# Building the FFN matrix from mirrored columns, in a cross-attention and Fourier-FFN kernel: a rewritten first row group

## The chip, the core and the metric

The kernel runs on one core of a Trainium2 chip. The core has five engines with instruction queues of their own, which run in order and meet only at semaphores: TensorE (PE in the profile, with PEld for its weight loads), VectorE (DVE), ScalarE (ACT), GpSimd (POOL) and SyncE (SP), which here only issues transfers (DMAs). The metric is the device time of one execution in microseconds (us). Everything is in float32.

## The reference

Two residual blocks over `x` of shape (2, 2048, 512), with a context of (2, 128, 512):

```python
x = x + xattn(layernorm(x), ctx, mask, wq, bq, wk, bk, wv, bv, wo, bo)
x = x + ffn(layernorm(x), w_freq_real, w_freq_imag, bias)
```

The cross-attention has 16 heads of 32. Scores are scaled, multiplied by the mask, and set to -1e9 where the product is zero; then softmax over 128 keys, the weighted values, and the output projection. The FFN works on frequencies:

```python
y = real(ifft(fft(x) @ (w_real + 1j * w_imag))) + bias
```

This is linear in `x`, so it is one real 512 x 512 matrix applied to each row. The kernel computes that matrix on the chip, from the two weight matrices and cosine and sine tables, and then uses it as an ordinary weight.

## The kernel before, in words

**Tiling.** The 4096 rows are eight groups of 512 (`GQ`), each of four tiles of 128. Group i, tile t is written (i,t). One tile's attention is a "slot" (`slot`, L687): the scores of 16 heads in two halves of eight (`scores`, L297; matmul L307), then for each half the mask multiply (`masked`, L326), the compare and the row minima (`maxima`, L333 to L336) on VectorE, eight exponentials with sums on ScalarE (`exponentials`, L342), a reciprocal on VectorE and the division on GpSimd (`divided`, L354, L355). TensorE transposes the divided weights one tile later (`transposed_weights`, L368), in two halves of eight transposes, and ScalarE copies them out (L375).

**What fills TensorE.** A slot takes three "chains": products of 128 rows by 512 columns summed over four chunks (`chain`, L192 to L199; its matmul is L196 whatever the product is). Chains make queries (`q`), values (`v`), the output projection (`o`), the FFN (`y`), and, in the first groups, the two steps that build the FFN matrix (`half`, `m`). Group i's slots carry the queries of the next group, the projection of group i-1 and the FFN of group i-2.

**What sets the order.** The program's order is written out by hand (a manual schedule): each engine's queue holds its instructions in the order in which the Python code issues them. Tiles of on-chip memory come from pools with few buffers, and an instruction that takes a buffer waits for its last user. Those that matter here: `ps_mm` ("mm", two buffers for the results of chains), `ps_tp` ("tp", two, for transposes), `ps_sc` ("sc", two, the halves of a tile's scores), `rel` (four, one for each row tile of a group).

**The start.** SyncE issues all loads in one order: context, rows of group 0, key and query bias, wq, rows of group 1, the mask of group 0, the FFN weights wr and wi, wv, the tables (`dft`), wo (L139 to L178 of the code). `keys` (L507) transposes the context and forms the keys, with "busy" transposes of the identity (L505) before and between; ScalarE evicts the keys (L547). Rows are reduced to differences from their first element (`relative`, L228), reduced to statistics (`query_statistics`, L203 to L208), normalized (`query_norm`, L211) and transposed (`query_transposes`, L186). Then TensorE makes all four query chains of group 0 (`Queries`, the first in two halves of 256 columns at L276), with three folds between, before the first scores.

**The FFN matrix.** `FoldRows` (L585) adds and subtracts the rows of wr and wi whose frequencies mirror each other: one matmul with a flipped identity (L597), up to four operations on VectorE (L604 to L611). `fold_columns` (L615) does the same for columns, with four 510-wide VectorE operations, one operand of each read backwards (L628), and four copies of an unpaired column (L629). `Half` (L631) multiplies these columns with the tables, four chains of 512 columns; `FfnMatrix` (L655) multiplies the result with the tables again, four more. Each is evicted by one ScalarE instruction (L651, L668). The row without a mirror partner sits in the place of the sine row that is zero: L856 sets that row of the table to ones. The two `half` tables' columns are the even (cosine) and odd (sine) functions of the column number.

Group 0 runs in the same loop as groups 1 to 5: values and queries of group 1 in its slots 0 and 1, `half` in slots 2 and 3, `m` from slot (0,3) to (1,1).

Of the kernel before, what the change touches and what calls it, by code (L numbers as in the profile page):

```python
# [9 lines left out]
FP = mybir.dt.float32  # L10
# [12 lines left out]
def kernel(  # L23
# [130 lines left out]
    nc.sync.dma_start(wq, chunks(wq_w))  # L154
    load_rows(1)
    load_mask(0)
# [35 lines left out]
    def chain(name, lhs, rhs):  # L192

        ps = ps_mm.tile([P, D], FP, tag="mm", name=name)
        for c in range(NC):
            nc.tensor.matmul(  # L196
                ps, lhs(c), rhs(c), start=(c == 0), stop=(c == NC - 1)
            )
        return ps  # L199
# [30 lines left out]

    def query_statistics(i, first, end):
# [23 lines left out]
    class Queries:  # L255
        def __init__(self, i, g):
            self.i, self.g = i, g

        def pe(self):
            i, g = self.i, self.g  # L260
            if g == 0:
                qTs[i] = big_tile("qT", 2, f"qT_{i}")
            if i > 0 or g > 0:
                self.ps = chain(
                    f"q_{i}_{g}",
                    lambda c: wq[:, c, g * P : (g + 1) * P],
                    lambda c: xnTs[i][:, c, :],
                )
                return


            self.ps = ps_mm.tile([P, GQ], FP, tag="mm", name="q_0_0")
            for h in range(2):
                qs = slice(h * GQ // 2, (h + 1) * GQ // 2)
                for c in range(NC):
                    nc.tensor.matmul(  # L276
                        self.ps[:, qs],
                        wq[:, c, :P],
                        xnTs[i][:, c, qs],
                        start=(c == 0),  # L280
                        stop=(c == NC - 1),
                    )

        def evict(self):
            nc.scalar.activation(  # L285
                qTs[self.i][:, self.g, :],
                self.ps,
                AF.Identity,
                bias=bq[:, self.g : self.g + 1],
            )  # L290
# [210 lines left out]
    def busy(count):  # L501

        ps = ps_tp.tile([P, NC, P], FP, tag="tp", name=f"busy_{count}")
        for k in range(count):
            nc.tensor.transpose(ps[:, k % NC, :], ident, ident)  # L505

    def keys():  # L507
# [11 lines left out]
        busy(2)  # L519
# [25 lines left out]
        def evict():  # L545
            for g in range(NC):
                nc.scalar.activation(  # L547
                    kT[:, g, :],
                    ps[g],
                    AF.Identity,  # L550
                    bias=bk[:, g : g + 1],
                    scale=SCALE / UNIT,
# [4 lines left out]
    class Values:  # L557
# [13 lines left out]
        on_vector = True  # L571

# [42 lines left out]
    def fold_columns():  # L615
# [4 lines left out]
        for k, (x1, x2, op, first) in enumerate(  # L620
# [7 lines left out]
            nc.vector.tensor_tensor(cols[:, k, :, 1:], x1, x2, op)  # L628
            nc.vector.tensor_copy(cols[:, k, :, 0:1], first)  # L629

    class Half:  # L631


        def __init__(self, what, g):
            self.what, self.g = what, g

        def pe(self):
            what, g = self.what, self.g
            self.ps = chain(
                f"half_{what}_{g}",  # L640
                lambda i: cols[
                    :,
                    2 * what + i // HC,
                    HC - 1 - i if i < HC else i - HC,
                    g * P : (g + 1) * P,
                ],
                lambda i: dft[:, i, :],
            )

        def evict(self):  # L650
            nc.scalar.copy(half[:, self.what * HC + self.g, :], self.ps)  # L651

        on_vector = False

    class FfnMatrix:  # L655
        def __init__(self, g):
            self.g = g

        def pe(self):
            g = self.g  # L660
            self.ps = chain(
                f"m_{g}",
                lambda i: half[:, i, g * P : (g + 1) * P],
                lambda i: dft[:, i, :],
            )

        def evict(self):
            nc.scalar.mul(m_ffn[:, self.g, :], self.ps, 1.0 / D)  # L668

        on_vector = False  # L670
# [110 lines left out]
    evict_biases()  # L781
    for t in range(TG):
        query_transposes(0, t)
        relative(1, t, nc.gpsimd)
    evict_keys()
    query_statistics(1, 0, TG)
    for t in range(TG):
        query_norm(1, t)
# [5 lines left out]
    for g in range(NC):  # L794
        run(Queries(0, g))
        if g > 0:
            run(folds[g - 1])

    halves_of = [Half(what, g) for what in range(2) for g in range(HC)]
    m = [FfnMatrix(g) for g in range(NC)]  # L800
    none = [None] * TG

    for i in range(last - 1):
# [3 lines left out]
        o = [Project(p, t) for t in range(TG)] if p >= 0 else none  # L807
        f_pp = [Ffn(pp, t) for t in range(TG)] if pp >= 0 else none
        f_p = Ffn(p, 0) if p >= 0 else None
        if i == 0:  # L810
            first, second = [Values(0), Values(1), q[0]], [q[1], q[2], q[3]]
            third, fourth = halves_of[:3], [halves_of[3], m[0], q_nn]
        else:
            if i == 1:
                first, second = [m[1], m[2], q[1]], [q[2], q[3], m[3]]
            else:
                first, second = [f_pp[1], f_pp[2], q[1]], [q[2], q[3], f_pp[3]]
            third, fourth = o[:3], [o[3], f_p, q_nn]

        def behind(*work):  # L820
            return list(work) if p >= 0 else []

        def before(*work):
            return list(work) if pp >= 0 else []

        load_rows(nn)
        load_mask(n)
        call(before((load_residual, p)))
        slot(
            i,  # L830
            0,
            first,
            turned=(p, TG - 1) if p >= 0 else None,
            early=(
                [(query_transposes, n, t) for t in range(TG)]
                if i == 0
                else before((ffn_transposes, pp, 1), (ffn_transposes, pp, 2))
            ),
            pool=[(relative, nn, t, nc.gpsimd) for t in range(TG)],
            on_b=before((ffn_norm, pp, 3)) + [(query_statistics, nn, 0, 2)],  # L840
            on_c=[(query_statistics, nn, 2, TG)],
            end=[(run, folds[3])] if i == 0 else [(context, p, 0, 2)],
        )
# [5 lines left out]
            early=behind((context, p, 2, NC)) + before((ffn_transposes, pp, 3)),  # L849
            pool=behind((output_bias, p)) if p > 0 else [],  # L850
            on_b=[(query_norm, nn, 0), (query_norm, nn, 1)]
            + ([(fold_columns,)] if i == 0 else []),
        )
        if i == 0:
            load_residual(0)
            nc.vector.memset(dft[0:1, HC, :], 1.0)  # L856
# [3 lines left out]
            third,  # L860
            turned=(i, 1),
            early=[(query_transposes, nn, 0), (query_transposes, nn, 1)],
            pool=behind((output_bias, p)) if p == 0 else [],
            on_b=behind((ffn_statistics, p, 0))
            + [(query_norm, nn, 2), (query_norm, nn, 3)]
            + behind((ffn_norm, p, 0)),
# [179 lines left out]
```

## Time and profile before

| what | value |
|---|---|
| median of three runs | 555.21 us (555.14 to 557.09) |
| the profiled execution | 557.46 us, span of its instructions 555.5 us |
| DVE, ACT, POOL busy | 430.3 us (77%), 344.0 us (62%), 316.3 us (57%) |
| share of PE in the chain that ended last | 81% |
| scores of (0,0), (0,1), (0,2), (0,3) begin | 35.38, 50.10, 63.46, 77.64 us |
| scores of (1,0), (1,1), (1,2) begin | 91.82, 107.42, 122.63 us |
| division of a half's weights on POOL (L355) | 1921 ns, 64 times |
| bias added to a row tile on POOL (L406) | 1520 ns, 32 times |

A group of instructions in the profile is one line, engine, operation and pair of tiles; it comes with its busy time, the mean of one instruction, and what ended the idle time before it. Matmul records overlap in TensorE's pipeline, so a busy PE row says that something was in flight, and the price of a matmul is better read from the starts of consecutive rows in the timeline. Records count two for one float32 matmul; a transpose is one.

### The profile page before, as it was taken

The page shows a single profiled execution, that of the slowest core. Times are in us where ns is not written, and L with a number is a line of the kernel's source. Part 1 is how long each engine was busy: PE and PEld are TensorE (multiplying, and loading weights), DVE is VectorE, ACT ScalarE, POOL GpSimd, SP SyncE. Part 2 cuts the span into 40 slices and gives each one's busy share as a digit, 9 for nine tenths or more (in the row PEclk, how much of TensorE's full clock was granted, in tenths as well). Part 3 has the DMA queues.
Part 4 walks back from the last instruction along what each step waited for, and adds up shares of the span by engine and source line. Part 5 has one row for each costly group of instructions (what it writes and reads, how often), then busy time and mean ns, then how long its engine had stood idle before and what let it go on. Part 6 is the DMA issues. An engine that isn't in the chain of part 4 may idle for free.

```text
span 555.5 us, 8688 instructions
## 1 busy us (share of the span) xinstructions
PE 543.2 (98%) x2975; PEld 291.4 (52%) x2975; DVE 430.3 (77%) x613; ACT 344.0 (62%) x1295; POOL 316.3 (57%) x248
## 2 busy tenths in 40 slices
PE   8999999999999999999999999999999999998997
PEld 7654555455554555455545555455545555454444
DVE  4468986669997898879898898879857898798251
ACT  3325777876766666777666666677776666666200
POOL 3534224727697268944696259935645466855450
PEclk9999999999999999999999999999999999999999
DMA  8950130000150005000230006000310201201102
GB/s 325 378 187 2 48 104 21 0 1 1 35 194 0 21 1 197 31 6 14 99 129 1 21 1 209 21 19 1 114 38 23 73 2 58 94 2 38 40 0 76
DMA packets 22735, 36.47 MB, mean 66 GB/s; under 512 B 1946, under 2 KB 6306, under 8 KB 22692
## 3 DMA queue, kind: packets, MB, share of 16 engines
q1 hardware_dynamic: 22004, 34.75, 18.0%
q10 hardware_dynamic: 688, 1.18, 0.6%
q8 instruction: 23, 0.38, 0.3%
q14 instruction: 20, 0.16, 0.1%
HBM read 27.53 MB, written 8.39 MB: 65 GB/s over the span
## 4 chain that ended last, share of the span: by engine, by line
PE 81%; DVE 10%; ACT 6%; issue 1%; DMA 1%; POOL 1%; SPq 0%; ACTq 0%; DVEq 0%; POOLq 0%
PE q L196 18%; PE y L196 16%; PE o L196 15%; PE tpw L368 8%; PE sc L307 5%; PE c L390 5%; ACT w L342 4%; DVE w L333 3%; PE half L196 2%; DVE nmax L335 2%; PE tp_a L186 2%; PE tp_f L186 2%; PE m L196 2%; DVE w L326 2%; PE k L533 2%; PE v L196 1%
## 5 line engine op out<-in xcount | busy, mean ns | idle before, releaser
L342 ACT ACTIVATE w<-w,nmax 128x128 f32<-128x128 f32 x512 | 198.3, 396 | 16.6 <-DVE nmax L336 14.7
L355 POOL TENSOR_TENSOR w<-w,rden 128x1024 f32<-128x1024 f32 x64 | 123.0, 1921 | 144.0 <-DVE rden L354 81.7
L196 PE MATMUL o<-wo,cT 128*128 128x512 f32 x256 | 115.1, 594 | 0.0
L196 PE MATMUL y<-m_ffn,nT 128*128 128x512 f32 x248 | 112.3, 596 | 2.1 <-DVE nT L190 1.0
L196 PE MATMUL q<-xnT,wq 128*128 128x512 f32 x248 | 112.1, 594 | 0.0
L375 ACT COPY pt<-tpw 128x512 f32<-128x512 f32 x124 | 66.7, 587 | 65.0 <-PE tpw L368 65.0
L342 ACT ACTIVATION_READ_ACCUMULATOR w<-w,nmax 128x1 f32 x512 | 99.5, 194 | 0.0
L333 DVE SCALAR_TENSOR_TENSOR w<-w 128x1024 f32<-128x1024 f32 x64 | 89.1, 1393 | 1.0
L326 DVE TENSOR_TENSOR w<-sc,mask 128x1024 f32<-128x1024 f32 x64 | 77.5, 1212 | 9.5 <-PE sc L307 9.0
L335 DVE TENSOR_REDUCE nmax<-w 128x8 f32<-128x1024 f32 x64 | 78.1, 1220 | 2.2
L368 PEld LDWEIGHTS tpw<-ident,w 128*128 128x128 f32 x512 | 59.5, 141 | 36.0 <-issue 31.2
L196 PEld LDWEIGHTS o<-wo,cT 128*128 128x128 f32 x256 | 46.3, 190 | 47.9 <-issue 46.6
L196 PEld LDWEIGHTS y<-m_ffn,nT 128*128 128x128 f32 x248 | 44.7, 190 | 48.3 <-issue 44.8
L368 PE MATMUL tpw<-ident,w 128*128 128x128 f32 x512 | 67.9, 274 | 2.0 <-ACT nT L188 1.0
L196 PEld LDWEIGHTS q<-xnT,wq 128*128 128x128 f32 x248 | 44.8, 190 | 47.6 <-issue 44.7
L445 POOL TENSOR_TENSOR x<-x,bf 128x512 f32<-128x512 f32 x32 | 48.9, 1528 | 18.0 <-DVE norm_f L211 18.0
L228 POOL TENSOR_SCALAR rel<-rows 128x512 f32<-128x512 f32 x28 | 46.7, 1681 | 15.1 <-PE tp_a L186 15.1
L354 DVE RECIPROCAL rden<-den 128x8 f32<-128x8 f32 x64 | 12.7, 199 | 54.2 <-ACT w L342 54.1
L406 POOL TENSOR_TENSOR x<-x,bo 128x512 f32<-128x512 f32 x32 | 47.6, 1520 | 0.0
L307 PEld LDWEIGHTS sc<-kT,qT 32*128 32x128 f32 x1024 | 31.4, 186 | 22.4 <-issue 20.0
L285 ACT ACTIVATE qT<-q,bq 128x512 f32<-128x512 f32 x32 | 21.7, 678 | 32.0 <-PE q L196 30.5
L207 POOL TENSOR_SCALAR rstd_f<-mv_f 128x1 f32<-128x1 f32 x32 | 19.9, 623 | 34.8 <-DVE mv_f L204 34.8
(81 smaller groups left out, 526.2 us busy)
## 6 DMA issues: line engine op xcount, KB each, us to landing
rows<-in_x_dram SPq DMA_DIRECT2D x32, 256.0 KB, 4.5
x<-in_x_dram SPq DMA_DIRECT2D x32, 256.0 KB, 4.9
out_dram<-x SPq DMA_DIRECT2D x31, 256.0 KB, 2.0
mask<-in_mask_Bx1xSxS_fk_dram SPq DMA_DIRECT2D x8, 256.0 KB, 4.8
wk<-in_L_xattn_wk_w_dram ACTq DMA_DIRECT2D x2, 512.0 KB, 6.5
wq<-in_L_xattn_wq_w_dram SPq DMA_DIRECT2D x1, 1024.0 KB, 7.2
wr<-n_L_ffn_w_freq_real_dram SPq DMA_DIRECT2D x2, 512.0 KB, 5.3
wi<-n_L_ffn_w_freq_imag_dram SPq DMA_DIRECT2D x2, 512.0 KB, 6.6
```

The lines of the kernel that those rows point to most:

```text
L196: nc.tensor.matmul(ps, lhs(c), rhs(c), start=(c == 0), stop=(c == NC - 1))
L228: eng.tensor_scalar(d, xt, xt[:, 0:1], None, ALU.subtract)
L307: nc.tensor.matmul(sc[r // 2][:, r % 2, g, :], qTs[i][rows, g, t * P : (t + 1) * P], kT[rows, g, b * K : (b + 1) * K], start=True, stop=True,)
L326: nc.vector.tensor_tensor(self.w, self.sc.rearrange("p r g k -> p (r g) k"), self.mrow, ALU.mult)
L333: nc.vector.scalar_tensor_tensor(w, w, 0.0, w, ALU.is_equal, ALU.subtract)
L335: nc.vector.tensor_reduce(self.nmax, w, AX.X, ALU.min)
L342: nc.scalar.activation(w[:, h, :], w[:, h, :], AF.Exp, bias=self.nmax[:, h : h + 1], scale=-UNIT, accum_out=self.den[:, h : h + 1],)
L355: nc.gpsimd.tensor_tensor(w, w, rden.unsqueeze(2).to_broadcast([P, HH, K]), ALU.mult)
L368: nc.tensor.transpose(ps[:, r, :], ws[r // 2].w[:, (r % 2) * NC + g, :], ident)
L375: nc.scalar.copy(dst, ps)
L406: nc.gpsimd.tensor_tensor(xs[:, t, :], xs[:, t, :], bo, ALU.add)
L445: nc.gpsimd.tensor_tensor(xt, xt, bf, ALU.add)
```

## The change

- **Mirrored sums.** `Half` and `FfnMatrix` become one class, `Mirrored`. Of each chain of four matmuls, two make the even part (257 columns) and two the odd part (255). ScalarE evicts the even part with a bias and the odd part to a tile of its own; two operations then form the columns above 256, backwards, as even minus odd, and the columns below as even plus odd. They run on GpSimd for seven of the eight sums and on VectorE, from the accumulator, for the fourth `half`.
- **The unpaired row.** It is now a bias for each partition. Four transfers of 128 elements gather the row into a [4, 128] tile, TensorE transposes it and ScalarE copies it, once for `half` and once for `m`. The row of ones in the table is gone.
- **Columns.** `fold_columns` runs on GpSimd, in tile (0,2). The first `half` stands in tile (0,3) instead of (0,2), and the last `m` in (1,0) instead of (1,1). The projection of group 0 begins in (1,2) as before.
- **Queries ahead.** The queries of the first tile alone (128 columns) stand before the first scores; the other 384 columns of group 0 follow in tile (0,0). Row tile 3 is transposed after the first queries.
- **Order at the start.** Keys are evicted by VectorE. Two of group 1's subtractions move from GpSimd to VectorE. The mask of group 0 is loaded ahead of the rows of group 1. Two filler transposes after the context's become three after each half of it, in the "mm" pool.
- **Group 0 and slot (1,0)** are written out one by one. Folds stand in tiles (0,0) and (0,1). In (1,0), the first two weight copies and the first two context evictions go to VectorE. The loop runs from group 1, and its code from slot (1,1) on is what it was, but for the three chains of (1,1), now q_1, q_2, q_3.

```diff
-    load_rows(1)
     load_mask(0)
+    load_rows(1)
...
+    def first_queries(i, g):
...
+        ps = chain(
+            f"q_{i}_{g}_first",
+            lambda c: wq[:, c, g * P : (g + 1) * P],
+            lambda c: xnTs[i][:, c, :P],
+            width=P,
+        )
...
+        nc.scalar.activation(
+            qTs[i][:, g, :P], ps, AF.Identity, bias=bq[:, g : g + 1]
+        )
...
-                nc.scalar.activation(
+                nc.vector.tensor_scalar(
                     kT[:, g, :],
                     ps[g],
...
-            nc.vector.tensor_tensor(cols[:, k, :, 1:], x1, x2, op)
-            nc.vector.tensor_copy(cols[:, k, :, 0:1], first)
+            nc.gpsimd.tensor_tensor(cols[:, k, :, 1:], x1, x2, op)
+            nc.gpsimd.tensor_copy(cols[:, k, :, 0:1], first)
...
+    def load_first_rows(name, pieces):
+
+        rows = small.tile([NC, P], FP, tag="rows0", bufs=2, name=name)
+        for k, piece in enumerate(pieces):
+            nc.sync.dma_start(rows[k : k + 1, :], piece)
+        return rows
+
+    def first_rows(name, rows, scale):
+
+        ps = ps_tp.tile([P, NC], FP, tag="tp", name=f"ps_{name}")
+        nc.tensor.transpose(ps, rows, ident[:NC, :NC])
+        add = small.tile([P, NC], FP, tag="add", bufs=2, name=name)
+        nc.scalar.mul(add, ps, scale)
+        return add
+
+    class Mirrored:
...
+        def pe(self):
+            ps = ps_mm.tile([P, D], FP, tag="mm", name=self.name)
+            self.even, self.odd = ps[:, : HD + 1], ps[:, HD + 1 :]
+            for i in range(NC):
+                nc.tensor.matmul(
+                    self.even if i < HC else self.odd,
+                    self.lhs(i),
+                    dft[:, i, : HD + 1] if i < HC else dft[:, i, 1:HD],
+                    start=(i % HC == 0),
+                    stop=(i % HC == HC - 1),
+                )
+
+        def evict(self, add, eng=nc.gpsimd):
+            low, high = self.dst[:, 1:HD], self.dst[:, D - 1 : HD : -1]
+            nc.scalar.activation(
+                self.dst[:, : HD + 1],
+                self.even,
+                AF.Identity,
+                bias=add,
+                scale=self.scale,
+            )
+            odd = self.odd
+            if eng is nc.gpsimd:
+                odd = work.tile([P, HD - 1], FP, tag="odd", name=f"odd_{self.name}")
+                nc.scalar.mul(odd, self.odd, self.scale)
+            eng.tensor_tensor(high, low, odd, ALU.subtract)
+            eng.tensor_tensor(low, low, odd, ALU.add)
...
+    for t in range(TG - 1):
+        query_transposes(0, t)
+    evict_keys()
     for t in range(TG):
...
+        relative(1, t, nc.gpsimd if t < 2 else nc.vector)
+    query_statistics(1, 0, TG - 1)
+    for g in range(NC):
+        first_queries(0, g)
+    query_transposes(0, TG - 1)
...
+    w = begin(0, 0)
+    w[0].masked()
+    run(rest[0])
+    w[0].maxima()
+    query_statistics(1, TG - 1, TG)
+    w[0].exponentials()
+    w[1].masked()
+    run(rest[1])
+    run(rest[2])
+    w[1].maxima()
+    w[1].exponentials()
+    run(rest[3])
+    for t in range(TG):
+        query_norm(1, t)
+    w[0].divided()
+    run(folds[0])
+    w[1].divided()
+    run(folds[1])
...
+    w = begin(0, 2)
+    w[0].masked()
+    fold_columns()
+    rows_h = load_first_rows("rows_h", [x.lhs(HC)[0:1, :] for x in h])
+    load_residual(0)
...
+    w = begin(0, 3)
+    w[0].masked()
+    q[2].evict()
+    w[0].maxima()
+    add = first_rows("add_half", rows_h, 1.0)
+    for k in range(HC):
+        h[k].pe()
+        h[k].evict(add[:, k : k + 1])
+    transposed_weights(0, 2, 0, HC)
+    w[0].exponentials()
+    w[1].masked()
...
+    h[2].pe()
+    h[2].evict(add[:, 2:3])
+    rows_m = load_first_rows("rows_m", [x.lhs(HC)[0:1, :] for x in m])
+    h[3].pe()
+    h[3].evict(add[:, 3:4], nc.vector)
+    transposed_weights(0, 2, HC, NC)
+    w[1].exponentials()
+    w[0].divided()
+    run(q[3])
+    m[0].pe()
+    add = first_rows("add_m", rows_m, 1.0 / D)
+    m[0].evict(add[:, 0:1])
+    w[1].divided()
```

## The prediction, made before the changed kernel was run

> **What bounds the kernel now.** I read the page first, then the groups by shape in the first 140 us, the timeline of PE, the waits of PE, and small windows for the first matmuls. The page:
>
> ```profile
> span 555.5 us, 8688 instructions
> ...
> PE 543.2 (98%) x2975; PEld 291.4 (52%) x2975; DVE 430.3 (77%) x613; ACT 344.0 (62%) x1295; POOL 316.3 (57%) x248
> ...
> PE   8999999999999999999999999999999999998997
> ```
>
> PE is busy from end to end, and in the first 140 us its waits are few:
>
> ```profile
> PE tp_enc L513 <- DMA enc<-in_ctx_dram: 0.6, 1, 0.6
> PE tp_a L186 <- ACT xnT L188: 0.5, 2, 0.3
> ...
> PE c L390 <- ACT qT L285: 0.2, 1, 0.2
> ```
>
> So PE work taken out of the start shortens the span, until another queue is late. The groups of that stage (columns: busy us, mean ns | idle before):
>
> ```profile
> L196 PE MATMUL m<-dft,half 128*128 128x512 f32 x32 | 14.5, 596 | 0.0
> L196 PE MATMUL half<-dft,cols 128*128 128x512 f32 x32 | 14.4, 593 | 0.0
> ...
> L276 PE MATMUL q<-xnT,wq 128*128 128x256 f32 x16 | 3.6, 379 | 0.0
> ...
> L333 DVE SCALAR_TENSOR_TENSOR w<-w 128x1024 f32<-128x1024 f32 x14 | 19.8, 1417 | 0.4
> ...
> L211 DVE TENSOR_SCALAR rel<-rel,mv,rstd 128x512 f32<-128x512 f32 x16 | 13.0, 856 | 1.9 <-POOL rstd L208 1.9
> ...
> L628 DVE TENSOR_TENSOR cols<-wr 128x510 f32<-128x510 f32 x2 | 1.4, 677 | 0.0
> ```
>
> Matmul records overlap, so their mean is not their price; that is the distance between starts, read from the timeline of PE:
>
> ```profile
> 18.58 3.62 PE L276 MATMUL q<-xnT,wq 128*128 128x256 f32 x16
> 22.03 3.60 PE L196 MATMUL q<-xnT,wq 128*128 128x512 f32 x8
> ```
>
> Sixteen records of 256 columns take 3.45 us (0.216 each); eight of 512 take 25.47 - 22.03 = 3.44 (0.43 each). Time goes with columns. The kernel's records are two per fp32 matmul, so a chain of four is eight records.
>
> **PE's saving.** Eight chains (four half, four m) go from 512 columns to 257 and 255: 8 x 0.216 = 1.73 us for 3.44. That is 8 x 1.71 = 13.7 us. Two small transposes of the unpaired row add 0.1 each. The split queries cost nothing: 4 x (8 x 0.109, the spacing of 128-column transposes) + 4 x (8 x 0.323) = 13.8, against 3.45 + 3 x 3.44 = 13.8. Net 13.5 us, if nothing waits.
>
> **The new order, walked queue by queue.** Both kernels have done the same work where the scores of tile (1,2) begin: 122.63 in the trace of before (q_1 of group 2 has moved behind, m_3 ahead). I price PE's work from the end of the keys (16.3) to there: scores 1.10, half a tile's weight transposes 0.87, four transposes 0.45, a fold 0.86, two context groups 1.85. For before the prices sum to 103.5, with 0.7 of waits; the trace has 106.3. The missing 2.1 are joints (a chain behind scores takes 3.63, not 3.44); the new order has as many, so I add 2.1 to it too. The other queues: DVE 3.8 for one half's mask, compare and reduce; 0.87 for a row tile's statistics; ACT 3.1 for eight exponentials, 0.55 to 0.7 for a 512-wide eviction.
>
> *To the first scores.* Transposes of three tiles and a wait for ACT (0.4): 18.1. First queries 3.5, tile 3's transpose 0.45: scores at 22.2, against 35.4. The key evictions move to DVE, 4 x 0.42, done by 18.1, covered by the first queries; without that cover they would cost 1.7. DVE has a new wait: the subtraction for row tile 3 of group 1 takes a buffer that PE frees with tile 3's transpose (22.1). Three statistics (2.6) and then the first mask multiply are queued behind it, so softmax begins at 25.2, not 23.3.
>
> *Tile (0,0)*: PE 1.1 + 4 x 2.59 + 2 x 0.86 = 13.2. PE has two product buffers, and ACT frees them in order. DVE ends the first half at 29.0, the second at 33.8 (one statistic between), so exponentials run 29.0 to 32.1 and 33.8 to 36.9. Rest-query 1's eviction stands behind the first: rest-query 3 waits 1.5. Rest-query 3's stands behind the second: the second fold waits 1.2. Then norms and two folds keep DVE until 40.1.
>
> *Tile (0,1)*: 1.1 + 1.8 + 2 x 3.44 + 2 x 0.87 + 2 x 0.86 = 13.2, and 0.3 for ACT. DVE has 13.1 here, as much as PE, and ends at 54.8.
>
> *Tile (0,2)*: 1.1 + 3 x 3.44 + 2 x 0.87 = 13.2. DVE: 54.8 + 2 x 3.8 + 1.7 of statistics = 64.3; last exponentials to 67.4.
>
> *Tile (0,3)*: 1.1 + 5 x 1.73 + 3.44 + 1.74 + 0.2 = 15.1. ACT has no gap to speak of from 67.4: query, unpaired row and two sums to 70.8, weight copies 72.2, exponentials 75.3, two sums and copies 77.7, exponentials 80.8, last query 81.5. PE waits 0.7 for half_2's eviction and 0.7 for that query.
>
> *Tile (1,0)*: 1.1 + 5.2 + 1.8 + 1.74 + 3.44 + 1.85 = 15.1. *(1,1)*: 1.1 + 1.85 + 10.3 + 1.74 = 15.0.
>
> Sum: 5.3 before the scores, 84.8 in six tiles, 2.1 of joints, 4.8 of waits: 97.0, so (1,2) at 113.3, 9.3 ahead: 13.5 saved, 4.8 of new waits, 0.7 of old ones gone. Scores (1,0) come near 82 (before 91.8). From (1,2) on the code is the same and PE has no slack to give back, so the lead is carried to the end.
>
> **Moved to GpSimd.** No row shows a mirrored operand on it. The nearest, x + bo of 512 (1.27 to 1.52), gives some 1.4 for 510 and 0.8 for 255; bounds: 1.1 and 0.6 below, three times the rows above. A mirrored operand cost DVE nothing (L628 0.68, the same as its plain 512-wide adds), so I take the rows. Columns: 4 x (1.4 + 0.25) = 6.6, 55.3 to 62.3 (with a release): the first half matmul needs them at 66.4, so hidden by 4; what is next late is the unpaired row's transfers. Fourteen adds for seven sums: 11 us, and the weights' divisions of tiles 2 and 3 queue between them; the weights of (0,2) are divided by 69.5 (67.6 + 1.9) and transposed at 70; those of (0,3) by 85.9, behind m_0's adds, transposed at 88. ACT evicts each sum in two pieces of 0.39 for one of 0.58: +0.2 each, covered except in tile (0,3), where it is in the walk. DVE loses 3.4 of columns and takes 0.8 for half_3, and in (1,0) two weight copies and two context evictions, 2.4 in all, from ACT: 13.9 in that tile under PE's 15.1.
>
> **Transfers.** Eight of 512 B. Nearest rows: 2.0 us to landing (out, lightly loaded) to 4.5 (rows). The first four wait for the columns and land at 65 to 67.5, wanted at 66.1; the other four wait for half_2 (77.6) and land at 81 to 83.5, wanted by PE at 81, with the scores of (1,0) queued behind. I take 2.0, since the queues are idle then; at 4.5 it costs 1.4 + 2.5. On SP, the first residual load stands behind the first four (used after 100) and rows and mask of later groups behind the last four (rows used at 89): covered. Mask 0 ahead of rows 1 delays those by one 256 KB transfer, 0.7 us, under 22.1.
>
> [...] Rows: L211 takes 0.48 alone (four in 1.92 at 25.67) and 0.86 on average; L333 1.23 alone and 1.42. [...] The added GpSimd work meets about six L333 and four L211: by the rows 6 x 0.2 + 4 x 0.38 = 2.7 us of DVE[...]. I take the rows, a third of it (0.9) on the path, since only (0,3) of the three tiles it meets is without slack[...]. Lead: 9.3 - 0.9 = 8.4.
>
> The keys' windows (count of matmul records in each us; the granted clock reads 1.00 throughout):
>
> ```profile
> 9.00:10.00 1.00, 1.00 (x4) 0.75 (x3) 0.00 (x0) 1.00 0.99 330
> ...
> 12.00:13.00 1.00, 1.00 (x7) 0.87 (x6) 0.00 (x0) 1.00 1.06 406
> ```
>
> PE runs at half pace until about 10.8. [...] The added filler transposes close the 0.56 us hole at 5.0[...]. I take nothing and keep 1.5 for the range.
>
> **Against the clock.** The profiled execution took 557.46 (span 555.5, 2.0 around it), 2.25 above the median 555.21 of runs from 555.14 to 557.09. The sum is a difference, so I take it off both: 549.1 for an execution like the profiled one, and 555.2 - 8.4 = 546.8 for the median.
>
> **The rivals.**
> - *Waits vanish* (0.20): the queues overlap better than in my in-order walk[...]. Lead 13.5 without waits, 541.7[...]. For it: ACT is only 62% busy. Against: two product buffers.
> - *DVE takes PE's place in group 0* (0.20): it has 14 to 15.5 us in tile (0,0) and 13.1 in (0,1), starts late[...]. Lead 3.8: 551.4; slow transfers end there too.
> - *Mirrored operands are slow on GpSimd* (0.04): three times the rows. Columns 4 x 2.8 more, less 2.0 of cover before the transfers are late: 9 on the path; the adds of half_2 and the m chain behind it some 6. 546.8 + 15 = 562. It decides against the kernel from about 3.1 us for a 510-wide operation (8.4 + 2.0 of cover over 4 + 6/2.8 a microsecond). Against it: DVE's 0.68.
> - *Halving the columns does not halve the time* at odd widths (0.03): lead under 3, 553.5. Against it: 0.216 for 256.
>
> **The numbers.** The likeliest is the lead of 8.4 (0.53; 544 to 549.5). The range 541.0 to 552.0 leaves out the last two rivals and the edges of the others. About 0.5% (2.8 us) is what a measurement of this kernel can tell from no change: faster 0.89, same 0.07, slower 0.04.
>
> **What would show it.** PE: half and m at about 1.73 us a chain; scores (0,0) near 22, (1,0) near 82 to 83, (1,2) near 114. GpSimd cols near 1.4 each. DVE waiting for tp_a of tile 3 near 22; PE waiting for ACT qT in tile (0,0). Wrong if PE's waits before (1,2) sum above 8 us, if cols exceed 2 us, or if PE idles more in the unchanged later groups.

## The result, and the profile after

| | before | after |
|---|---|---|
| median | 555.27 us (555.14 to 557.09, 4 executions) | 546.71 us (546.47 to 546.90, 4 executions) |
| ratio | | 0.9838, 95% interval 0.9817 to 0.9859 |
| profiled execution, span | 557.46, 555.5 us | 546.47, 544.7 us |

The change saves 8.6 us, 1.6%. The page of after, in the rows that were shown of before:

```profile
span 544.7 us, 8783 instructions
...
PE 528.8 (97%) x3005; PEld 292.7 (54%) x3005; DVE 431.5 (79%) x616; ACT 342.9 (63%) x1300; POOL 329.5 (61%) x268
...
PE   8989999999999999999999999999999999998997
```

PE has 14.4 us less to do than on the page of before, and the row of tenths has gained one 8, in slice 3 (27 to 41 us): there PE now waits. The waits of PE in the first 130 us of after (total, times, longest):

```profile
PE q L196 <- ACT qT L287: 1.5, 1, 1.5
...
PE q L196 <- ACT odd_half L693: 1.0, 1, 1.0
PE low_wr L602 <- ACT qT L287: 0.9, 1, 0.9
PE tp_a L186 <- ACT xnT L188: 0.5, 2, 0.3
PE tpw L370 <- POOL m_ffn L695: 0.5, 1, 0.5
```

All but the fourth are new. The two of `qT` stand in tile (0,0), behind the exponentials; that of `odd_half` in tile (0,3), behind half_2's eviction. The groups by shape, for the same 130 us (busy us, mean ns | idle before; those of before in the prediction are for 140 us):

```profile
L335 DVE SCALAR_TENSOR_TENSOR w<-w 128x1024 f32<-128x1024 f32 x15 | 22.6, 1505 | 0.3
...
L211 DVE TENSOR_SCALAR rel<-rel,mv,rstd 128x512 f32<-128x512 f32 x16 | 10.5, 696 | 0.5 <-POOL rstd L208 0.5
...
L673 PE MATMUL half<-dft,cols 128*128 128x257 f32 x16 | 4.3, 393 | 0.1
...
L633 POOL TENSOR_TENSOR cols<-wr 128x510 f32<-128x510 f32 x2 | 2.6, 1276 | 0.0
```

The columns take 1.09 to 1.28 us each on GpSimd. The compare (L335, L333 of before) has become slower, 1.51 for 1.42; the normalization (L211) has become faster, 0.70 for 0.86. The price of a matmul is again in the starts, here on the timeline of PE: two mirrored sums (sixteen records of 257 and 255 columns) and the query chain behind them.

```profile
69.79 3.62 PE L673 MATMUL half<-dft,cols 128*128 128x257 f32 x16
...
75.23 3.70 PE L196 MATMUL q<-xnT,wq 128*128 128x512 f32 x8 [0.96 <-ACT odd_half L693]
```

The two sums end their records' starts at 73.24, so a sum takes 1.73 us, where a full chain takes 3.44. And the keys, by windows of 1 us (count of matmul records):

```profile
7.00:8.00 1.00, 1.00 (x5) 0.87 (x6) 0.00 (x0) 1.00 1.04 393
8.00:9.00 1.00, 1.00 (x6) 0.90 (x5) 0.00 (x0) 1.00 1.07 389
9.00:10.00 1.00, 1.00 (x7) 0.87 (x6) 0.00 (x0) 1.00 0.95 306
```

They run at full pace from 7 us on (5 to 7 records in each us); in the profile of before they ran at half pace until 10.8 (2 to 4 in each us from 7 on). That profiled execution took 557.46 us, 2.2 above the median, so the marks of after are compared below with a second profile of before, which does not have the half-paced start (experiment 1).

### The profile page after: what moved, and what is told of

It is laid out like the page before. It is cut to its first block, busy times and chain, and to the rows that moved or that the text cites. A ratio compares the mean times of both kernels' runs of the same rounds, so it can differ in the third digit from the quotient of the medians.

```text
span 544.7 us, 8783 instructions
## 1 busy us (share of the span) xinstructions
PE 528.8 (97%) x3005; PEld 292.7 (54%) x3005; DVE 431.5 (79%) x616; ACT 342.9 (63%) x1300; POOL 329.5 (61%) x268
## 4 chain that ended last, share of the span: by engine, by line
PE 79%; DVE 11%; ACT 6%; POOL 1%; issue 1%; DMA 1%; SPq 0%; ACTq 0%; DVEq 0%; POOLq 0%
PE o L196 18%; PE y L196 17%; PE q L196 16%; PE tpw L370 8%; PE sc L309 5%; PE c L392 5%; ACT w L344 4%; DVE w L335 3%; DVE nmax L337 2%; PE tp_f L186 2%; DVE w L328 2%; PE tp_a L186 2%; PE k L535 1%; PE v L196 1%; DMA enc<-in_ctx_dram 1%
## 5 line engine op out<-in xcount | busy, mean ns | idle before, releaser
L196 PE MATMUL q<-xnT,wq 128*128 128x512 f32 (+1 forms) x256 | 112.0, 582 | 2.6 <-ACT qT L287 1.5
L377 ACT COPY pt<-tpw 128x512 f32<-128x512 f32 x122 | 65.6, 587 | 65.2 <-PE tpw L370 65.2
L335 DVE SCALAR_TENSOR_TENSOR w<-w 128x1024 f32<-128x1024 f32 x64 | 89.8, 1404 | 0.9
L196 PEld LDWEIGHTS q<-xnT,wq 128*128 128x128 f32 x256 | 46.3, 190 | 48.6 <-issue 40.2
L228 POOL TENSOR_SCALAR rel<-rows 128x512 f32<-128x512 f32 x26 | 42.0, 1630 | 1.2 <-PE tp_a L186 1.2
L188 ACT COPY nT<-tp_f 128x512 f32<-128x512 f32 x30 | 17.1, 585 | 34.5 <-PE tp_f L186 34.4
```

Of the source, the lines that this page charges most:

```text
L196: nc.tensor.matmul(ps, lhs(c), rhs(c), start=(c == 0), stop=(c == NC - 1))
L228: eng.tensor_scalar(d, xt, xt[:, 0:1], None, ALU.subtract)
L335: nc.vector.scalar_tensor_tensor(w, w, 0.0, w, ALU.is_equal, ALU.subtract)
L377: nc.scalar.copy(dst, ps)
```

## The experiments

Each run is timed beside before on its own chip; ratios are to before. The medians of before on these chips were 555.26, 555.27, 555.29 and 555.65, so two kernels from different chips are told apart here by their medians only to some tenths of a us.

### 1. Before, once more

The kernel before, unchanged, for a profile of a usual execution.

> The kernel before, unchanged. In its first profile the 32 matmul records of the keys took 9.1 us (PE at half pace until 10.8), in the profile after 7.5 us, and the profiled execution of before was 2.2 us above its median. If the half pace is a matter of each execution's luck, an execution of 555.2 us shows the keys in about 7.5 us and one of 557.3 us shows them in 9.1 us. If the changed fillers made the difference, the keys take 9.1 us here whatever the total is.

Measured: 555.27 us (555.11 to 557.39), ratio 0.9993 (0.9981 to 1.0006). The profiled execution took 555.35 (span 553.3), and its keys run at full pace. The waits of PE in its first 130 us are those of the first profile. This is the profile to set against after. Scores begin at (us; of the last row take 2.1 off, see experiment 4):

| tile | (0,0) | (0,1) | (0,2) | (0,3) | (1,0) | (1,1) | (1,2) |
|---|---|---|---|---|---|---|---|
| before, this profile | 33.18 | 47.91 | 61.27 | 75.45 | 89.63 | 105.23 | 120.44 |
| after | 20.05 | 36.33 | 50.24 | 63.84 | 80.76 | 96.76 | 111.97 |
| full chains in the new order (3) | 20.09 | 36.37 | 50.27 | 63.87 | 87.52 | 108.48 | 123.69 |
| mirrored sums in the old order (4) | 35.26 | 49.99 | 63.34 | 74.02 | 94.30 | 108.98 | 122.48 |

After leads by 8.47 us at (1,2), and by 8.6 at the end. What was gained was gained by (1,2), and none of it is given back.

### 2. The fillers: alone, and left out

```diff
-        ps = ps_tp.tile([P, NC, P], FP, tag="tp", name=f"busy_{count}")
+        ps = ps_mm.tile([P, NC, P], FP, tag="mm", name="busy")
...
-        busy(2)
+            busy(3)
```

This diff alone, put into before:

> The kernel before with the new filler transposes alone (three after each half of the context, in the product pool). Luck theory: no change of the median, 555.2, ratio 1.000. Filler theory: the keys take 7.5 us in every profile and the median falls by up to 2 us, to 553.3.

Measured: 555.42 us (555.06 to 555.69, 12 executions), ratio 0.9993 (0.9984 to 1.0002). And after with this diff taken back:

> The changed kernel with the old two filler transposes. Luck theory: 546.7 as the changed kernel, with an execution near 548.8 now and then. Filler theory: 548.8 in the median, 2.1 above the changed kernel.

Measured: 546.80 us (546.76 to 548.60, 4 executions), ratio 0.9843 (0.982 to 0.9865).

What follows: the fillers do not move the median. They very likely do away with the occasional execution that is 2 us longer. With the old ones, 13 of 97 executions of before in this study were above 556.5 us; with the new ones none of 37 executions of seven kernels was off its kernel's median by more than 0.6. (The twelve of this experiment alone would not show it.) That the longer executions are those with half-paced keys rests on the profiles: the first one of before (557.46) has them, and those at 555.35 and 555.26 have not; the 13 were not profiled.

### 3. The new order with full chains

The mirrored sums are undone in after: four matmuls of 512 columns, one eviction, the row of ones in the table, no transfers and no sums on GpSimd.

```diff
-            ps = ps_mm.tile([P, D], FP, tag="mm", name=self.name)
...
+            self.ps = chain(self.name, self.lhs, lambda i: dft[:, i, :])
...
-            eng.tensor_tensor(high, low, odd, ALU.subtract)
-            eng.tensor_tensor(low, low, odd, ALU.add)
+            nc.scalar.mul(self.dst, self.ps, self.scale)
```

> The changed kernel with the mirrored sums undone alone: chains of 512 columns, one eviction each, the row of ones in the table, no sums on GpSimd and no transfers of the unpaired row. Theory of the PE sum: 13.5 us of PE work come back and the waits in tiles (0,3) and (1,0), 1.5 us, mostly vanish: 546.7 + 13.5 - 1.5 = 558.7, so 3.5 us slower than before; the new order by itself costs its waits of tile (0,0). Rival, that the earlier softmax is itself a gain: below 555.

Measured: 558.82 us (558.80 to 558.92), ratio 1.0052 (1.0034 to 1.0069). Within the new order the mirrored sums are worth 558.82 - 546.71 = 12.1 us of the 8 x 1.71 = 13.7 they take off PE. By itself the new order, and with it all that is not the sums (the columns on GpSimd, the split queries), costs 3.5 us (2.9 by the ratio on its own chip): its tile (0,0) waits as after does (1.48 and 0.93 us).

### 4. The mirrored sums in the old order

The other half of the change alone: before, with `Mirrored` for `Half` and `FfnMatrix` in their old places, the additions of all eight sums on GpSimd, the unpaired row by transfers, the columns left on VectorE. Beside the order, then, it differs from after in the columns and in the fourth `half`, which after adds on VectorE.

```diff
-    halves_of = [Half(what, g) for what in range(2) for g in range(HC)]
-    m = [FfnMatrix(g) for g in range(NC)]
+    halves_of = [
+        Mirrored("half", what * HC + g, cols_of(what, g), half[:, what * HC + g, :], 1.0)
+        for what in range(2)
+        for g in range(HC)
+    ]
+    m = [Mirrored("m", g, half_of(g), m_ffn[:, g, :], 1.0 / D) for g in range(NC)]
```

> The kernel before in its own order, with the mirrored sums alone: the same places for half and m, columns on VectorE as before, every sum's two operations on GpSimd, the unpaired row by transfers. PE loses 13.7 us in four tiles, and the next engine sets each tile. ScalarE has in (0,2) row copies 1.1, weight copies 2.35, exponentials 6.3 and three sums 2.6 = 12.3 (PE had 14.2), in (0,3) 13.5 (14.2), in (1,0) 12.3 (15.6), and PE itself has 13.5 in (1,1) (15.2). Theory that the sums alone carry the gain: 1.9 + 0.7 + 3.3 + 1.7 = 7.6, 547.7. Rival, that the new order is what lets the gain through: the first sum then waits for the unpaired row's transfers and the tiles for ScalarE and VectorE, 551 or more.

Measured: 557.48 us (555.43 to 558.85, 18 executions), ratio 1.0034 (1.0022 to 1.0045). The theory that the sums alone carry the gain (547.7) failed, and its rival (551 or more) holds: of a gain of 12 us in the new order nothing is left in the old one; the fastest of the 18 executions, 555.43, is no faster than the median of before. The profiled execution is one of the slowest (558.67), and its keys are half-paced (5 and 7 matmul records in the 2 us from 7 and from 9, for 10 and 11 in experiment 1): its scores of (0,0) begin 2.1 us late, long before the first sum. Up to (0,3) the sums do pay: tile (0,2) takes 10.7 us and not 14.2. Then tile (0,3) takes 20.3 us for 14.2. With 2.1 taken off, (1,2) begins at 120.4, as in before (120.44); another 1.3 us is lost up to (2,0), where PE now waits 1.2 us for a normalization on VectorE (0.5 before) and twice 0.4 for other work of VectorE. Why the executions spread over 3.4 us is open; the mean clock does not order them (0.994 at 555.43 and at 558.75). The chain of waits through tile (0,3), in order of time (start, us):

```profile
76.87 1.75 ACT w L342 x9
...
78.64 0.21 DVE rden L354
...
78.99 1.90 POOL w L355
80.89 1.68 POOL half L689
...
82.63 0.73 POOL half L690
...
83.38 0.50 SPq L648
...
83.93 0.59 SPq L648
...
84.56 0.59 SPq L648
...
85.19 1.71 DMA m<-half
...
87.04 0.24 PE ps_m L653
87.28 1.90 PE tpw L368 x8
89.18 5.19 PE q L196 x8
```

It reads as a relay: ScalarE ends the exponentials; their weights' division on GpSimd stands ahead of the half sums; SyncE issues the row's transfers one by one; they land; and PE, whose queue is in order, can only then go on to the weights and the query chain that stand behind the row's transposition. PE idles for 5 us in the stretch from 78 to 87. Two things stand out at its end. The query chain takes 5.19 us, where the same chain takes 3.44 elsewhere. And the granted clock was below 1.00 there (busy us and count of PE, clock, DMA share and GB/s, in stretches of 5 us):

```profile
75.00:80.00 5.00, 3.33 (x26) 1.00 0.00 0
80.00:85.00 5.00, 2.80 (x15) 1.00 0.01 2
85.00:90.00 5.00, 3.56 (x13) 0.58 0.52 158
90.00:95.00 5.00, 5.00 (x32) 0.74 0.33 106
95.00:100.00 5.00, 5.00 (x46) 1.00 0.02 3
```

The 0.58 and the 0.74 are means: in windows of 1 us the clock reads 1.00 up to 85, 0.50 from 86 to 92, and 1.00 from 93. So it fell to 0.50 after two stretches in which PE was busy for 6.1 of 10 us, and stayed there after PE was busy again; eight weight transposes took 1.76 us from start to start there (from 87.21), for 0.87 elsewhere. Every one of the 18 executions shows a mean clock below 1.00, most 0.994. The longest single wait in this tile was 1.44 us; in experiment 6 the clock fell behind one of 2.08. A longer one of this run, 2.68 us up to 107.99, left it at 1.00 (in the stretch from 105 to 110). What sets the fall is not shown.

### 5. Which link of that chain

Two kernels built on experiment 4. First, the transfers left out: the row is zeros, so two terms of the FFN matrix are missing.

```diff
-        for k, job in enumerate(jobs):
-            nc.sync.dma_start(rows[k : k + 1, :], job.lhs(HC)[0:1, :])
+        nc.gpsimd.memset(rows, 0.0)
```

> The order of before with the mirrored sums (557.48 us, granted clock 0.994 in every execution), and the unpaired row left out: its eight small transfers are gone, zeros stand in their place, so two of the terms of the FFN matrix are missing. Theory A, the transfers hold PE up: the two waits for them (1.3 us for the halves' row, 1.4 us for the matrix's row) go, and since the second is the last link of the chain behind which the clock fell to 0.58, most of the 3.3 us lost to the clock (0.006 of 534 busy us) goes too: 551.5 to 553.5. Theory B, the hold comes from the chain ACT eviction, GpSimd division, GpSimd sum, and the transfers only end it: at most the 1.4 us return and the clock stays at 0.994 to 0.997: 555 to 557.

Measured: 556.34 us (555.31 to 558.52, 20 executions), ratio 1.002 (1.001 to 1.003); clock 0.991 to 0.994. At most 1.1 us return (the intervals of the two ratios overlap), and the clock does not. Theory A falls, and the time is what B expected, at a clock a little lower: the transfers end the relay, but do not make it. The profiled execution (557.96, span 556.1) is slower than the median by 1.6, but begins with full-paced keys and can be set against experiment 1. It has 6.9 us less PE work (533.9 for 540.8) and 9.7 us more idle (22.2 for 12.5), which is its 2.8 us. Of the 13.7 us that the sums take off PE, the clock takes back up to 0.009 x 534 = 4.8 in this execution, by estimate, and up to 3.2 in those at 0.994; how much of that a wait would have taken anyway is not shown. Its waits, in the stretch from 20 to 130 us:

```profile
PE c L390 <- ACT qT L285: 3.0, 1, 3.0
PE m L666 <- POOL half L689: 1.6, 2, 0.9
PE tpw L368 <- ACT xnT L188: 1.4, 1, 1.4
PE tpw L368 <- POOL w L355: 1.1, 2, 0.7
```

They wait for ScalarE and for GpSimd, and 0.9 us more for VectorE. The largest, in tile (1,0), is a context product that wants a buffer whose query is evicted behind the exponentials; before, it was 0.2.

Second, idle time filled with transposes that nobody reads, to keep the clock up.

```diff
+        for k in range(18):
+            nc.tensor.transpose(ps[:, 1 + k % (NC - 1), :], ident, ident)
...
+                if self.name == "m_0" and i == HC:
+                    for _ in range(10):
+                        nc.tensor.transpose(self.odd[:, :P], ident, ident)
```

> The order of before with the mirrored sums, and transposes of the identity on PE, whose results nobody reads, where it idled in tile (0,3): 10 ahead of the odd sums of m_0 (about 0.6 us, in a wait of 0.7) and 18 ahead of the transposition of each unpaired row (about 1.1 us, in waits of 1.3 and 1.4). Theory C, the clock eats the gain: with those idles filled the granted clock stays near 1.00, the query chain behind them takes 3.5 us and not 5.4, and the time falls by the 3.3 us that the clock cost: 554.2. Theory D, the waits alone eat it, and the slow query chain is hidden by later waits for ACT (the context waits 2.7 us at 108): the time stays within 0.7 us of 557.5 although the clock is back.

Measured: 556.82 us (555.73 to 560.68, 16 executions), ratio 1.0023 (1.0011 to 1.0036); clock mostly 0.997. This settles little. The query chain did come back to 3.53 us, but the fillers were mis-sized: I had reckoned 0.06 us a transpose, an estimate that no row shows, where the prediction had already read 0.109; they took 0.11, and 0.21 for the ten in m_0, which fell into a stretch of clock 0.50 of their own. So they took 2.06, 2.14 and 2.06 us in holes of 1.3, 1.5 and 1.4, some 2 us too much, about what the query chain had won. And the profiled execution is the slowest of the sixteen (560.68): half-paced keys, and a mean clock of 0.991, since the clock fell a second time at 106 us, in a wait of 3.0 us (mean 0.82 from 100 to 110, 0.84 from 110 to 120). Neither C (554.2) nor D (no change) is shown. In fourteen of the other fifteen the mean clock is 0.997 for 0.994, so about half of the clock's loss came back there; the median fell by 0.7 us at most.

### 6. The columns on VectorE

After, with `fold_columns` back on VectorE, in its new place.

```diff
-            nc.gpsimd.tensor_tensor(cols[:, k, :, 1:], x1, x2, op)
-            nc.gpsimd.tensor_copy(cols[:, k, :, 0:1], first)
+            nc.vector.tensor_tensor(cols[:, k, :, 1:], x1, x2, op)
+            nc.vector.tensor_copy(cols[:, k, :, 0:1], first)
```

> The changed kernel with the columns formed on VectorE, in the same place. The chain of after runs on VectorE from 49.5 to 66.5. Theory of the walk: VectorE gets 3.3 us more there[...], so the lead falls by 2.7: 549.4. [...]

Measured: 549.26 us (549.21 to 549.42), ratio 0.9887 (0.987 to 0.9903). The move of the columns is worth 2.5 us, though GpSimd takes almost twice as long for each (1.23 us on average in after, for the 0.68 of VectorE in before). Expected were 2.7: 3.3 of moved work, less 0.6 as the author's estimate of what VectorE loses beside it (in after the compare that begins during the first column operation takes 1.84 us, for the 1.22 of the one at 24.21). VectorE sets the pace of softmax in tile (0,2), and what stands on it there delays ScalarE, in whose queue the sums' evictions wait: in the profile of this run PE waits 2.1 us in tile (0,3) for the copy of the unpaired row on ScalarE, a wait that after does not have.

```profile
64.84 1.99 PE L673 MATMUL half<-dft,cols 128*128 128x257 f32 x8
68.92 3.50 PE L673 MATMUL half<-dft,cols 128*128 128x257 f32 x8 [2.08 <-ACT add_half L659]
72.22 1.26 PE L370 MATMUL tpw<-ident,w 128*128 128x128 f32 x8
```

The sum behind the wait takes 3.30 us from start to start, and not 1.73: in windows of 1 us the clock reads 0.50 there, from 70 to 72. The clock does not seem to set the time, though: two of the four executions show a mean clock of 0.999 for 0.997, and took 549.21 and 549.23 us for 549.30 and 549.42.

### 7. Two waits of after, taken away

The prediction named two waits that the new order makes. First, the subtraction of group 1's row tile 3, which takes a buffer that PE frees late, and behind which the first mask multiply is queued on VectorE: it is moved behind the first maxima.

```diff
-        relative(1, t, nc.gpsimd if t < 2 else nc.vector)
+        if t < TG - 1:
+            relative(1, t, nc.gpsimd if t < 2 else nc.vector)
...
+    relative(1, TG - 1, nc.vector)
```

> The changed kernel with the subtraction for row tile 3 of group 1 put behind the first half's compare and minima on VectorE, so that the first mask multiply does not stand behind the wait for tile 3's transpose. Softmax begins at 21.2 us for 22.97, the second exponentials end 1.3 earlier. Theory that this wait is on the path: 545.4. Rival, that VectorE and ScalarE in tiles (0,2) and (0,3) absorb it: 546.5.

Measured: 545.63 us (545.20 to 546.21), ratio 0.9821 (0.9804 to 0.9838). Second, the rest queries 1 and 3 are evicted ahead of the exponentials behind which they stood on ScalarE.

```diff
     w[0].maxima()
...
+    run(rest[1])
     w[0].exponentials()
     w[1].masked()
-    run(rest[1])
```

> The changed kernel with the evictions of rest queries 1 and 3 put ahead of the exponentials that they stood behind. PE's waits of 1.5 and 0.9 in tile (0,0) vanish, the exponentials of the second half start 0.9 later, the first mask multiply of (0,1) comes 1.2 earlier. Theory that these waits are on the path: 545.5. Rival, absorbed later: 546.5 to 547.

Measured: 545.97 us (545.72 to 546.25), ratio 0.9827 (0.981 to 0.9843). Both waits of `qT` are gone, 2.4 us, and the scores of (0,1) begin 2.8 us sooner, at 33.57; but those of (0,2) only 1.4 sooner (48.82) and those of (1,0) 0.8 (79.92). PE's gain met VectorE, which has as much to do in tile (0,1): PE now waits 1.1 us there for a copy of weights on ScalarE, behind exponentials that wait for VectorE, and 0.7 us at the start of (0,2) for a fold on VectorE. No execution of either kernel overlaps with those of after (546.47 to 546.90). Then both together:

> The kernel after with both improvements: the subtraction of the last row tile of the next mask table behind the first maxima on VectorE (alone 545.63) and the evictions of the rest queries 1 and 3 ahead of the exponentials on ACT (alone 545.97). If the two waits they take away lie one behind the other on the path (0.08 + 0.08 of a chance to overlap left out): 546.71 - 1.1 - 0.7 = 544.9. If the earlier first exponentials, which the first change brings, now run into the eviction put ahead of them (rest query 1 is written at about 26 to 27 us), part of the gain is lost: 545.5.

Measured: 544.61 us (544.54 to 545.06), ratio 0.9809 (0.9794 to 0.9823). The gains add: 1.1 + 0.7 was expected, 2.1 came. It is the fastest kernel of this study. The waits of PE that it still has up to (1,2), apart from the start's (of `tp_a`, one of the two is the start's):

```profile
PE q L196 <- ACT odd_half L693: 1.0, 1, 1.0
PE q L196 <- DVE wi L612: 0.7, 1, 0.7
PE tp_a L186 <- ACT xnT L188: 0.5, 2, 0.3
PE tpw L370 <- POOL m_ffn L695: 0.5, 1, 0.5
```

Not tried: the split queries alone, and the written-out slot (1,0) alone. The 3.5 us that the new order costs by itself are not divided among its parts.

## Why the prediction was right

546.8 was predicted and 546.71 measured; the lead was to be 8.4 and is 8.6. The mechanism was right: PE's work falls, and a part of it comes back as waits, mostly for ScalarE and in the tiles that were named. That the number fits within 0.2 us is luck, since two sizes were off by 1.5 and 1.6 us and cancel. None of the three signs of being wrong came: PE's waits before (1,2) sum to 6.3 us, the start's included, the columns stay under 1.3, and the later groups give nothing back. By its steps:

- **Halving the columns halves the time.** Right: 1.73 us a sum for 3.44, as priced. The rival that odd widths would not halve falls.
- **PE's saving, 13.5.** A little large. Between experiment 1 and after, PE's busy time falls by 12.0 us (540.8 to 528.8). The sums take off 13.1 of it (541.9 in experiment 3, whose busy time is otherwise the same work); the new order adds 1.1, where the prediction put it at nothing. Four more fillers are about 0.4 of it; the rest was not split.
- **New waits, 4.8, less 0.7 of old ones, and 0.9 for VectorE's loss beside GpSimd: 5.0.** Too large as well. PE's idle time in the span grows by 3.4 us (12.5 to 15.9). 12.0 - 3.4 = 8.6. The four new waits of the trace sum to 3.9, and the 0.9 for VectorE's loss does not show. So the two errors, 1.5 in the saving and 1.6 in the waits, cancel.
- **The walk.** The marks of the prediction were in the frame of the first profile, whose keys end at 16.3; those of after end at 14.2. With 2.1 added, after has 22.15 for 22.2, 38.4 for 38.1, 82.9 for 82 to 83, and 114.1 for 113.3 plus the 0.9 of VectorE's loss. (VectorE's line in it does not add up: 40.1 and 13.1 of work make 53.2, not 54.8, and 54.8, 7.6 and 1.7 make 64.1, not 64.3. The later mark is the better one: in after VectorE is free for tile (0,2) at 53.29, which is 55.4 in that frame.) The waits in tile (0,0) are 1.5 and 0.9 for 1.5 and 1.2. In tile (0,3), 0.7 and 0.7 were foreseen; 1.0 came, and 0.5 in (1,0), where a weight transposition stands behind an m sum. The trace puts that one down to GpSimd's sum; ScalarE's copy ended at about the same time, so its releaser is open.
- **The first softmax.** Right that the subtraction holds it. On the timeline of VectorE:

```profile
20.16 0.48 DVE L228 TENSOR_SCALAR rel<-rows 128x512 f32<-128x512 f32 x1 [3.41 <-PE tp_a L186]
...
22.97 1.20 DVE L328 TENSOR_TENSOR w<-sc,mask 128x1024 f32<-128x1024 f32 x1
```

  22.97 + 2.1 is 25.1, for 25.2. Experiment 7 shows that this wait was worth 1.1 us.
- **Mirrored operands on GpSimd.** Right: 1.23 us on average for 510 columns (1.4 taken) and 0.73 for 255 (0.8), where it does not begin during a compare or a normalization of VectorE (1.71 when begun during the compare at 67.81, 1.00 during the normalizations at 75.94). The rival at 562 falls.
- **VectorE beside the added GpSimd work.** Not right. 2.7 us of VectorE were to be lost, 0.9 of them on the path, an estimate from the rows of before (there a compare that begins during a division, at 80.11, takes 1.89 us for 1.23). By the groups, fifteen compares lose 0.09 us each, 1.3 in all, and sixteen normalizations (L211) win 2.5 (10.5 us for 13.0); why they win was not tried. Of the two slowest compares only the first meets added work, a fold of the columns (54.03 to 55.30); the second begins during a division that before has too:

```profile
54.54 1.84 DVE L335 SCALAR_TENSOR_TENSOR w<-w 128x1024 f32<-128x1024 f32 x1
...
67.81 2.00 DVE L335 SCALAR_TENSOR_TENSOR w<-w 128x1024 f32<-128x1024 f32 x1
```

```profile
54.03 1.27 POOL L633 TENSOR_TENSOR cols<-wr 128x510 f32<-128x510 f32 x1
...
66.84 1.90 POOL L357 TENSOR_TENSOR w<-w,rden 128x1024 f32<-128x1024 f32 x1 [0.20 <-DVE rden L356]
```

- **The keys.** Nothing was taken for the fillers, and nothing is what they give at the median (experiment 2); the 1.5 us kept for the range was the author's estimate. Most executions of before seem to have full-paced keys already. Taking the difference off the median rather than off the profiled time was what kept this out of the forecast.
- **The rival that the waits vanish** (541.7) had something in it: 2.1 us of them do vanish with three moved lines (544.61), but only by edits that the change does not make. **VectorE as the bound** (551.4, from a lead of 3.8 that was the author's estimate) did not come true in after; it shows in experiments 6 and 7, whenever VectorE is given more to do or PE less.

What the prediction did not ask is what either half of the change does alone. It walked the two together, and its sum of a saving and of waits reads as if the saving belonged to the sums and the waits to the order. Experiments 3 and 4 show that it does not divide like that: the sums alone, in the old order, gain nothing.

## What to carry to other kernels

Work that is taken off the engine that bounds a kernel is worth its full time only where the queues that feed it have room at that place: the same 13.7 us of matmuls were worth 12.1 in one order and nothing in another, as far as the traces show because each shorter sum brought more small steps on ScalarE, GpSimd and SyncE, in queues behind long ones. (No single step was it: without SyncE's transfers nearly all of the loss remained.) Follow the result's own path (evict, add, gather, transpose) through every in-order queue, and put it where those queues are free before counting the gain. The clock fell to 0.50 behind waits of up to 1.44 us in experiment 4 and behind one of 2.08 in experiment 6; what such a stretch cost in all was not separated here.

## What the runs showed of the hardware

- The granted clock fell to 0.50 at 86 us, for some 6 us, without any wait above 1.44 us, after 10 us of which PE was busy for 6.1 (experiment 4); the query chain behind it took 5.19 us for 3.44. It fell to 0.50 for some 3 us behind a single wait of 2.08 us (experiment 6). It stayed at 1.00 through a wait of 2.68 us (experiment 4, up to 107.99), and in after, with waits of 1.47 and 0.94 us within 6 us.
- The half-paced keys of the first profile of before do not show in the clock column, which read 1.00 there; they show only in the counts of records (3 in the us from 8, for 6 in experiment 1).
- VectorE and GpSimd slowed each other's operations in after, in both directions and down to very small ones. GpSimd's timeline, two copies of equal size, and two halves of one sum:

```profile
55.24 1.19 POOL L634 COPY cols<-wr 128x2 f32<-128x2 f32 x1
...
57.59 0.18 POOL L634 COPY cols<-wi 128x2 f32<-128x2 f32 x1
...
68.69 1.71 POOL L694 TENSOR_TENSOR half<-half,odd_half 128x255 f32<-128x255 f32 x1
70.48 0.73 POOL L695 TENSOR_TENSOR half<-half,odd_half 128x255 f32<-128x255 f32 x1
```

  The slow ones begin during the two compares of VectorE shown above (54.54 to 56.38, and 67.81 to 69.81); each lasts about as long as the rest of that compare (1.14 and 1.12) and its own time (0.18 and 0.73) together. The compares are slow themselves, begun during an operation of GpSimd (54.03 to 55.30, and 66.84 to 68.74): 1.84 and 2.00 us, for the 1.22 of the one at 24.21, which has none beside it.
- Transfers of 512 B from one place on the chip to another landed after 1.7 to 2.3 us (medians of four); in experiment 4 their issue took 0.5 to 0.6 us each on SyncE, so that issuing four (2.4 us) took longer than landing one (1.7).
